# One layer of a four-layer gated stack on Trainium2: query projections placed ahead of scores, rounded rows transposed half a step later, product rows scaled on other engines

## The chip, the cores and the metric

The kernel runs on one core of a Trainium2 chip. The core has a matrix engine (TensorE, PE in the profile, with PEld for its weight loads), a vector engine (VectorE, DVE), an activation engine (ScalarE, ACT), a general-purpose engine (GpSimd, POOL) and a queue for transfers (SyncE, SP). Each engine executes its own instructions in the order in which the program lists them, and they wait for each other by semaphores. The metric is the device time of one execution in microseconds; the time before is 1705.65 us, the median of 3 runs (1699.48 to 1706.13).

## The reference, cut to what matters

Four layers, each an attention over a context and then a feed-forward part, are added to the rows x (8 batches of 256 rows with 128 features) behind a gate. The change touches layer 1:

```
# attention, per batch: 16 heads of 64, 256 queries, 512 keys
query = einsum('btd,dnh->bnth', q, w_query) + b_query
scores = einsum('bnth,bnsh->bnts', query, key_p) * scale
weights = softmax(scores, axis=-1)
attn = einsum('bnts,bnsh->bnth', weights, value)
out = einsum('bnth,ndh->btd', attn, w_projection) + b_projection
x = x + tanh(g_xattn[1]) * out           # q is layernorm(x)

# feed-forward: a product of rows and weights rounded to int8
lhs_scale = max(max(abs(lhs), axis=2), 1e-12) / 127      # per row
q_lhs = clip(round(lhs / lhs_scale), -127, 127)
acc = q_lhs @ q_rhs
x = x + tanh(g_ffn[1]) * (acc * lhs_scale * rhs_scale)   # lhs is layernorm(x)
```

## The kernel before

**The pipeline.** Layers 1 to 3 are one software pipeline (`pipeline`, L921). A unit is half the heads of one batch of one layer; there are 48 units, and each takes 4 steps. A step has two half steps, called A and B here. Three generators are advanced in step with each other: `prepare` (queries, operands) runs ahead by 8 steps, `largest` (row maxima of layers 2 and 3) by 4, and `attend` does the attention itself. Layer 1's preparation is done in steps 0 to 63 and its attention in steps 8 to 71, so both run together in steps 8 to 63. Work that is not tied to a half step waits in lists: `due` (run in A from the given step on), `soon` (run later in the same half step), and `front` and `back`, from each of which one piece is taken per half step (`some`, L1002). All instructions are kept in program order (`InOrder`, L36, and `mm` and `tp`, L866 to 873), so the order of the calls is the order on each engine.

**Layer 1's attention.** A half step handles one chunk of 128 queries for a pair of heads (`attend`, L1194). In order: the transposes of the weights of the chunk of two half steps ago, if there is one (`turn`, L994, which runs the function that `turned`, L1218, returns: 8 TensorE transposes into a buffer sc, ScalarE's copy into et, GpSimd's two additions k and total); this chunk's scores into another sc (two halves); VectorE's negated row maximum nm; and at the end of the half step ScalarE's two exponentials into a tile that the profile calls m (`exponentials`, L987). After both chunks of a pair have been transposed, the product with the values goes into av in the next A (`values_of_pair`, L1253). In the same half step the column sums follow, by ones, into av, then VectorE's reciprocal rec and the product aT. Of sc there are three buffers, of av one, and of pj one.

**The queries.** In B, after the scores, `prepare1` (L1142) projects the queries of a unit two units ahead into pj (the group pj<-xT,wb), and ScalarE copies them with the bias into qx.

**Row work of layer 1.** When a batch's eight pairs are done, `output1` (L1280) projects them through pj, adds them to x, and appends `int8(b)` (L1312) to `back`. That generator's pieces, one per half step, begin in an A: layernorm in four pieces (statistics on VectorE, the inverse root on GpSimd, the rows xn on VectorE), the scale of each row (ls and its inverse li), the rounding of one chunk of 128 rows (`rounded`, L1298: two VectorE operations r and one on GpSimd, ql), that of the other, then the transposes of ql into pj with ScalarE's copy qlT, an empty piece, and last the product pj<-qr,qlT. The product's pieces in the code before:

```
for c in range(2):
    nc.vector.scalar_tensor_tensor(
        y[:, c, :], po[:, c * D : (c + 1) * D], ls[:, c : c + 1], self.rsb,
        ALU.mult, ALU.mult,
    )
self.added(y, 2 * b)
```

Here y is the tile that the profile calls row, and rsb holds the weights' scale times the gate, the same for all rows. `added` (L1575) adds y to x on GpSimd. In `front`, `ahead` (L1062) prepares the next batch of layer 1: gathers by GpSimd, additions, layernorm, and `rows_turned` (L1073), which transposes xn through pj into xT. For layers 2 and 3 `ahead23` (L1080) does the like, and the pieces `project`, `values`, `mask`, `largest_rows` and `output23` use pj too.

Of the kernel before, what the change touches and what calls it, by code (L numbers as in the profile page):

```python
# [15 lines left out]
AF = mybir.ActivationFunctionType  # L16
ALU = mybir.AluOpType
AX = mybir.AxisListType

P = 128  # L20
NB, S, SK, D = 8, 256, 512, 128
# [10 lines left out]
def bcast(ap, shape):  # L32
    return ap.to_broadcast(list(shape))
# [15 lines left out]
class Flamingo:  # L49
# [871 lines left out]
    def pipeline(self):  # L921
        nc, tc = self.nc, self.tc
        with ExitStack() as st:
            PS = bass.MemoryType.PSUM
            self.p_sc = st.enter_context(tc.tile_pool(name="p_sc", bufs=3, space=PS))
            self.p_pj = st.enter_context(tc.tile_pool(name="p_pj", bufs=1, space=PS))
            self.p_av = st.enter_context(tc.tile_pool(name="p_av", bufs=1, space=PS))
            self.po = st.enter_context(tc.tile_pool(name="pipe", bufs=2))
            units = [(layer, b, g) for layer in (1, 2, 3) for b in range(NB) for g in range(2)]
            self.turns, self.exps = [], []  # L930
            self.due, self.soon, self.back, self.front, self.step, self.kept = [], [], [], [], 0, {}
            streams = {
                n: self.chain(f, units, wait)
                for n, f, wait in (("pr", self.prepare, 0), ("la", self.largest, 4), ("at", self.attend, 8))
            }
            self.fill_tile = lambda: self.t(self.po, "et", [P, 2, 2, S], bufs=6).rearrange(
                "p a b s -> p (a b s)"
            )[:, 0:SK]
            self.fill2(8)
            for _ in self.ahead(1, 0):  # L940
                pass
            for self.step in range(4 * len(units) + 12):

                next(streams["at"])
                self.run_due()
                next(streams["la"])
                self.run_soon()
                self.some(self.front)
                self.some(self.back)
                self.exponentials()  # L950
                next(streams["at"])
                next(streams["pr"])
                next(streams["la"])
                self.fill2(1)
                self.some(self.front)
                self.some(self.back)
                self.exponentials()
            while self.due or self.back:
                self.step += 1
                self.run_due()  # L960
                self.run_soon()
                self.some(self.back)
            self.ternary_end()
# [27 lines left out]
                self.nc.scalar.activation(p[:, z, :], ps[:, z, :], AF.Exp, bias=nm[:, z : z + 1])  # L991
        self.exps = []

    def turn(self, n):  # L994

        if len(self.turns) >= n:
            self.turns.pop(0)()

    def later(self, steps, f):
        self.due.append((self.step + steps, f))  # L1000
# [193 lines left out]
    def attend(self, n, layer, b, g):  # L1194
        if layer > 1:
            yield from self.attend23(n, layer, b, g)
            return
        nc = self.nc
        qT, kT, va = self.kept[n]
        aT = self.t(self.po, "aT", [P, 4, S], bufs=3)  # L1200
        self.kept["aT", g] = aT
        both = [self.kept["aT", 0], aT]
        for j in range(4):
            held = {}
            for c in range(2):
                self.turn(2)
                ps = self.sc()
                for z in range(2):
                    h = slice(64 * z, 64 * z + 64)
                    self.mm(ps[:, z, :], qT[h, j, c * P : (c + 1) * P], kT[h, j, :])  # L1210
                nm = self.t(self.po, "nm", [P, 2])
                nc.vector.tensor_reduce(nm, ps, AX.X, ALU.max, negate=True)
                p = self.t(self.po, "m4", [P, 4, S], bufs=3).rearrange("p (z k) s -> p z (k s)", z=2)
                self.exps.append((p, ps, nm))
                self.turns.append(self.turned(c, p, held, (b, 4 * g + j, va, both)))
                yield

    def turned(self, c, p, held, of_pair):  # L1218
# [93 lines left out]
    def int8(self, b):  # L1312
        nc = self.nc
        xn = self.t(self.po, "xn", [P, 2, D])
        yield from self.layernorm(2 * b, xn, self.nc.vector)
        ls = self.t(self.sm, "ls", [P, 2])
        li = self.t(self.sm, "li", [P, 2])
        self.absmax_scale(ls, li, xn)
        yield
        ql = self.t(self.po, "ql", [P, 2, D], BF16)  # L1320
        for c in range(2):
            self.rounded(ql[:, c, :], xn[:, c, :], li[:, c : c + 1], -127.0, 127.0)
            yield
        pt = self.pj16()
        for c in range(2):
            self.tp(pt[:, c * P : (c + 1) * P], ql[:, c, :], self.identb)
        qlT = self.t(self.po, "qlT", [P, S], BF16)
        nc.scalar.copy(qlT, pt[:, 0:S])
        yield
        yield  # L1330
        po = self.pj()
        y = self.t(self.rows, "row2", [P, 2, D])
        for c in range(2):
            self.mm(po[:, c * D : (c + 1) * D], qlT[:, c * P : (c + 1) * P], self.qr)
        for c in range(2):
            nc.vector.scalar_tensor_tensor(
                y[:, c, :], po[:, c * D : (c + 1) * D], ls[:, c : c + 1], self.rsb,
                ALU.mult, ALU.mult,
            )
        self.added(y, 2 * b)  # L1340


# [142 lines left out]
    def attend23(self, n, layer, b, g):  # L1485
        qx, kx, _ = self.kept[n]
        va = self.kept["va", layer, b]
        _, bk = self.kept["mask", layer, b]
        rows = 38 if layer == 2 else 34
        scale = 1.0 / math.sqrt(8.0) if layer == 2 else 128.0**-0.5  # L1490
        if g == 0:
            aT = self.t(self.po, "aT", [P, 4, S], bufs=3)
            self.kept["oS"] = aT[:, 0:2, :], aT[:, 2:4, :]
        oS, oN = self.kept["oS"]
        held = {}
        for j in range(4):
            for k2 in range(2):
                self.turn(1)
                ps = self.sc()
                for z in range(2):  # L1500
                    self.mm(
                        ps[:, z, :], self.identb,
                        bk[:, 2 * k2 : 2 * k2 + 2, :].rearrange("p k s -> p (k s)"), True, False,
                    )
                for c in range(2):
                    for z in range(2):
                        at = (2 * k2 + c) * P
                        self.mm(
                            ps[:, z, c * S : (c + 1) * S],
                            self.packed(kx, z, 0, rows)[:, j, at : at + P].bitcast(F32R),  # L1510
                            self.packed(qx, z, 0, rows)[:, j, :].bitcast(F32R), False, c == 1,
                        )
                held[j, k2] = self.weights(ps, scale)
                if k2 and j % 2:
                    self.later(1, self.values_of_four(layer, b, g, j // 2, held, va, oS, oN))
                yield
# [340 lines left out]
```

## Time and profile before

| | |
|---|---|
| median of 3 runs | 1705.65 us (1699.48 to 1706.13) |
| profiled execution | 1706.16 us, its span 1704.4 us |
| busy: TensorE | 1501.9 us, 88% of the span |
| busy: VectorE | 1135.8 us, 67% |
| busy: ScalarE | 891.8 us, 52% |
| busy: GpSimd | 737.9 us, 43% |
| mean granted TensorE clock | 0.950 |
| layer 1's attention | about 345 to 875 us |
| a plain step in it (transposes at 601.96 and at 609.04) | 7.08 us |
| its five whole batches, 400 to 760 us: TensorE busy | 338.64 of 360 us |
| the same: VectorE, ScalarE, GpSimd busy | 253.57, 214.43, 227.49 us |

Names like `pj<-xT,wb` say which tile is written from which; buffer numbers are left out. A bracket or a column "idle before" gives the time that the engine had nothing to do ahead of an instruction, and the engine and tile whose end released it. The granted clock is the share of the TensorE clock that the chip let through in a stretch.

### The profile page before, as it was taken

What the parts mean: (1) busy time and instruction counts of PE and PEld (TensorE: products, weight loads), DVE (VectorE), ACT (ScalarE), POOL (GpSimd) and SP (SyncE); (2) the same over time, 40 slices, a digit from 0 to 9 for tenths busy, and PEclk for the clock granted to TensorE, in tenths of its full rate; (3) what the DMA queues carried; (4) which work ended last, traced back from release to release, by engine and by line L of the source; (5) the groups of instructions that cost most, each with busy time, mean ns of one, the idle gap of its engine ahead of it and who ended that gap; (6) DMA issues with size and microseconds to landing.
All of it is one profiled execution on the core that took longest, in us unless ns stands there. A gap on an engine that the chain in (4) does not pass through costs nothing.

```text
span 1704.4 us, 33649 instructions
## 1 busy us (share of the span) xinstructions
PE 1501.9 (88%) x12560; PEld 801.6 (47%) x12560; DVE 1135.8 (67%) x2634; ACT 891.8 (52%) x1468; POOL 737.9 (43%) x1189
## 2 busy tenths in 40 slices
PE   5886778799899999999888898898899999899995
PEld 2332225256566565566553444444444455344442
DVE  6998652156776767767776765664755755677764
ACT  3453443466555556556444555555555455455543
POOL 5896312355665766666542132222322323433311
PEclk9898998999999999999999999999999899899997
DMA  5453442731221122122222331222211121222200
GB/s 200 149 174 122 160 163 94 245 119 53 80 73 59 58 79 76 57 75 71 43 90 71 81 72 48 53 58 50 60 34 46 45 54 28 60 60 61 61 21 26
DMA packets 64903, 137.54 MB, mean 81 GB/s; under 512 B 12114, under 2 KB 27619, under 8 KB 58084
## 3 DMA queue, kind: packets, MB, share of 16 engines
q1 hardware_dynamic: 62770, 131.70, 25.2%
q0 software_dynamic: 1536, 3.15, 1.1%
q8 instruction: 100, 1.64, 0.4%
q10 hardware_dynamic: 434, 0.54, 0.1%
q14 instruction: 63, 0.52, 0.1%
HBM read 83.44 MB, written 51.38 MB: 79 GB/s over the span
## 4 chain that ended last, share of the span: by engine, by line
PE 56%; DVE 14%; ACT 6%; issue 6%; POOL 5%; DMA 2%; SPq 1%; ACTq 0%; DVEq 0%; POOLq 0%
PE sc L868 26%; PE av L868 14%; PE pj L868 7%; PE sc L872 5%; DVE junk L46 5%; PE pj L872 3%; DVE rec L46 2%; ACT et L46 1%; DVE x L46 1%; POOL lnz L46 1%; ACT total L46 1%; ACT m L46 1%; DVE nm L46 1%; POOL xs L46 1%; ACT row L46 1%
## 5 line engine op out<-in xcount | busy, mean ns | idle before, releaser
L46 DVE CUSTOM_DVE_ANT_0 junk<-sc,m 128x512 bf16<-128x512 f32 x512 | 350.8, 685 | 44.2 <-PE sc L868 30.7
L46 ACT ACTIVATE et<-sc 128x1024 f32<-128x1024 f32 (+1 forms) x267 | 268.9, 1008 | 147.4 <-PE sc L868 142.6
L868 PE MATMUL sc<-kx,qx 64*128 64x512 f32 (+2 forms) x1024 | 272.0, 571 | 7.1 <-DVE mx L46 5.3
L868 PE MATMUL av<-et,va 128*64 128x128 f32 (+1 forms) x4096 | 268.0, 348 | 0.0
L868 PEld LDWEIGHTS av<-et,va 128*64 128x64 f32 (+1 forms) x4096 | 178.7, 129 | 96.3 <-issue 49.7
L46 POOL TENSOR_TENSOR k<-et 128x512 f32<-128x512 f32 x128 | 162.7, 1271 | 131.2 <-ACT et L46 130.5
L46 ACT ACTIVATE m<-sc,nm 128x512 f32<-128x512 f32 x256 | 162.1, 685 | 88.6 <-DVE nm L46 86.2
L46 DVE TENSOR_REDUCE nm<-sc 128x2 f32<-128x1024 f32 x128 | 156.2, 1220 | 65.5 <-PE sc L868 57.4
L868 PE MATMUL sc<-m,identb 128*128 128x512 bf16 x512 | 159.9, 395 | 19.9 <-DVE mx L46 11.9
L46 POOL TENSOR_TENSOR x<-row,x 128x256 f32<-128x256 f32 x76 | 55.4, 729 | 268.1 <-ACT row L46 262.5
L46 ACT COPY et<-sc 128x1024 f32<-128x1024 f32 x128 | 129.7, 1013 | 60.5 <-PE sc L872 60.4
L46 DVE RECIPROCAL rec<-av 128x256 f32<-128x256 f32 x64 | 112.3, 1754 | 53.6 <-PE av L868 53.6
L872 PE MATMUL sc<-c_f,m 128*128 128x128 f32 x1024 | 139.1, 279 | 3.4 <-ACT m L46 2.9
L868 PE MATMUL sc<-qx,kx 38*128 38x256 f32 (+1 forms) x1024 | 133.6, 340 | 0.4 <-DMA qx<-ms 0.4
L868 PEld LDWEIGHTS sc<-qx,kx 38*128 38x128 f32 (+1 forms) x1024 | 79.5, 192 | 114.7 <-issue 111.4
L872 PEld LDWEIGHTS sc<-c_f,m 128*128 128x128 f32 x1024 | 110.3, 141 | 45.9 <-issue 35.6
L868 PEld LDWEIGHTS sc<-kx,qx 64*128 64x128 f32 (+2 forms) x1024 | 87.8, 187 | 73.3 <-issue 45.9
L46 DVE SCALAR_TENSOR_TENSOR x<-sc,comb,x 128x128 f32<-128x128 f32 x128 | 39.0, 346 | 100.3 <-ACT row L46 100.3
L46 POOL TENSOR_TENSOR lnz<-lny 128x2 f32<-128x2 f32 (+1 forms) x129 | 25.1, 195 | 183.5 <-DVE lny L46 169.8
L46 ACT ACTIVATE total<-sc,f_b 128x512 f32<-128x512 f32 x64 | 44.0, 688 | 107.5 <-PE sc L868 107.5
L46 POOL TENSOR_TENSOR total<-k 128x256 f32<-128x256 f32 x128 | 93.2, 728 | 10.0
L46 DVE SCALAR_TENSOR_TENSOR ms<-pj,ms 4x256 fp32r<-4x256 f32 x64 | 26.4, 412 | 100.8 <-ACT ms L46 93.0
(274 smaller groups left out, 2319.2 us busy)
## 6 DMA issues: line engine op xcount, KB each, us to landing
kx<-k SPq DMA_DIRECT2D x16, 1024.0 KB
va<-v SPq DMA_DIRECT2D x16, 1024.0 KB
k<-fill SPq DMA_DIRECT2D x54, 256.0 KB
v<-fill SPq DMA_DIRECT2D x53, 256.0 KB
pd<-k SPq DMA_DIRECT2D x16, 512.0 KB
kx<-pd SPq DMA_DIRECT2D x64, 128.0 KB
kx<-pd SPq DMA_DIRECT2D x128, 64.0 KB
qx<-pd SPq DMA_DIRECT2D x128, 64.0 KB
```

What stands on the lines that cost most here:

```text
L46: return lambda *args, **kw: self.tc.keep_in_program_order(v(*args, **kw))
L868: self.nc.tensor.matmul(out, lhsT, rhs, start=start, stop=stop)
L872: self.tc.keep_in_program_order(self.nc.tensor.transpose(out, in_, ident))
```

## The change

Three things are changed. First, the transposes are called by the pipeline itself at the head of each half step, and in steps 0 to 63 the B half step advances `pr` (the queries) before `at` (the scores); from step 64 on `at` comes first as before. `turn` now keeps one entry per half step, empty where there is nothing to transpose, and runs the one of two half steps ago. Second, `int8` has one more empty piece between the rounding and the transposes of ql, so that these, qlT and the product each come a half step later, in the other kind of half step. Third, the product's rows are multiplied by the row's scale on ScalarE, reading pj, and by rsb on GpSimd, where VectorE did both in one operation per chunk.

```
@@ pipeline
             for self.step in range(4 * len(units) + 12):
 
+                self.turn()
                 next(streams["at"])
                 self.run_due()
                 next(streams["la"])
...
                 self.exponentials()
-                next(streams["at"])
-                next(streams["pr"])
+
+                self.turn()
+                for n in ("pr", "at") if self.step < 8 * NB else ("at", "pr"):
+                    next(streams[n])
                 next(streams["la"])
@@
-    def turn(self, n):
-
-        if len(self.turns) >= n:
-            self.turns.pop(0)()
+    def turn(self):
+
+        self.turns.append(None)
+        if len(self.turns) > 2 and (run := self.turns.pop(0)):
+            run()
@@ attend
             for c in range(2):
-                self.turn(2)
                 ps = self.sc()
...
-                self.turns.append(self.turned(c, p, held, (b, 4 * g + j, va, both)))
+                self.turns[-1] = self.turned(c, p, held, (b, 4 * g + j, va, both))
                 yield
@@ int8
             self.rounded(ql[:, c, :], xn[:, c, :], li[:, c : c + 1], -127.0, 127.0)
             yield
+        yield
         pt = self.pj16()
...
         for c in range(2):
-            nc.vector.scalar_tensor_tensor(
-                y[:, c, :], po[:, c * D : (c + 1) * D], ls[:, c : c + 1], self.rsb,
-                ALU.mult, ALU.mult,
+            nc.scalar.activation(
+                y[:, c, :], po[:, c * D : (c + 1) * D], AF.Copy, scale=ls[:, c : c + 1]
             )
+        nc.gpsimd.tensor_tensor(y, y, bcast(self.rsb.unsqueeze(1), [P, 2, D]), ALU.mult)
         self.added(y, 2 * b)
@@ attend23
             for k2 in range(2):
-                self.turn(1)
                 ps = self.sc()
```

## The prediction

> **What bounds the kernel now.** I read the page first, then the PE's list of waits, the PE's timeline of one batch, and the table of stretches for the granted clock.
>
> ```profile
> PE 1501.9 (88%) x12560; PEld 801.6 (47%) x12560; DVE 1135.8 (67%) x2634; ACT 891.8 (52%) x1468; POOL 737.9 (43%) x1189
> PE 56%; DVE 14%; ACT 6%; issue 6%; POOL 5%; DMA 2%; SPq 1%; ACTq 0%; DVEq 0%; POOLq 0%
> ```
>
> TensorE is 88% busy and is over half of the chain that ended last. Layer 1's attention runs from 345 to 875 us, so that is the stage to read. Its waits on PE between 400 and 760 us, which is five batches (the columns are the total, the count and the longest):
>
> ```profile
> PE pj L872 <- ACT qx L46: 6.8, 10, 0.8
> PE pj L872 <- POOL ql L46: 5.3, 5, 1.1
> PE sc L872 <- ACT m L46: 2.9, 5, 0.6
> PE pj L868 <- ACT qx L46: 2.9, 5, 0.6
> PE pj L872 <- DVE xn L46: 2.5, 5, 0.5
> PE av L868 <- POOL total L46: 1.1, 5, 0.2
> ```
>
> Each comes a whole number of times per batch, so one batch tells all. Its places, from PE's timeline of the third batch (start, duration, what; the bracket is the idle time before it):
>
> ```profile
> 574.70 1.09 PE L872 MATMUL sc<-c_f,m 128*128 128x128 f32 x8 [0.58 <-ACT m L46]
> 575.72 1.13 PE L868 MATMUL sc<-kx,qx 64*128 64x512 f32 x4
> 576.78 0.65 PE L868 MATMUL pj<-xT,wb 128*64 128x256 f32 x4
> 578.21 0.22 PE L872 MATMUL pj<-identb,ql 128*128 128x128 bf16 x1 [0.78 <-ACT qx L46]
> 579.48 0.23 PE L872 MATMUL pj<-identb,ql 128*128 128x128 bf16 x1 [1.05 <-POOL ql L46]
> ...
> 588.84 0.27 PE L868 MATMUL pj<-qr,qlT 128*128 128x128 bf16 x2 [0.57 <-ACT qx L46]
> ...
> 596.62 0.33 PE L872 MATMUL pj<-c_f,xn 128*128 128x128 f32 x1 [0.57 <-ACT qx L46]
> 597.44 0.33 PE L872 MATMUL pj<-c_f,xn 128*128 128x128 f32 x1 [0.49 <-DVE xn L46]
> ```
>
> There is one pj buffer. Whatever writes it right behind the queries waits until ScalarE has read them (qx). Outside these places PE has no idle time over 0.1 us: a plain step is 7.08 us (transposes at 601.96 and again at 609.04).
>
> The granted clock, in stretches of 3.41 us laid on the grid of its drops (columns: length, PE busy, PEld, DVE, ACT, POOL, clock, DMA):
>
> ```profile
> 512.26:515.67 3.41, 1.99 (x14) 1.18 (x13) 2.77 (x9) 1.82 (x5) 2.28 (x3) 1.00 0.00 0
> 515.67:519.08 3.41, 3.41 (x45) 2.70 (x44) 1.87 (x2) 2.20 (x4) 2.21 (x3) 1.00 0.02 5
> 577.12:580.53 3.41, 1.58 (x16) 0.98 (x12) 3.27 (x10) 1.82 (x4) 2.22 (x3) 1.00 0.21 87
> 580.53:583.94 3.41, 3.41 (x19) 1.91 (x20) 1.42 (x3) 1.66 (x3) 2.45 (x4) 0.50 0.00 0
> ```
>
> Where both waits of the int8 transposes (0.78 and 1.05) fall into one stretch, PE is busy for 1.58 of 3.41 us and the next stretch runs at half clock. Where they are split (busy 1.99, and 2.30 from 645.38) it does not. Stretches starting at 444.00 and 710.24 are like 577.12: 1.58 busy, then 0.50. From the second int8 transposes to the first row transposes a batch with such a drop takes 17.14 us (579.48 to 596.62), one without 15.52 (513.89 to 529.41): a drop costs 1.62 us.
>
> **The sum's base.** The profiled execution: 1706.16 us (span 1704.4 and 1.8 around it), 0.5 above the median 1705.65.
>
> **Queries ahead of scores, 56 half steps (steps 8 to 63).** No instruction is added; in the built order PE alone changes places. Queries take 0.59 us start to start (576.78's group, from 604.04 to 604.63), scores 1.06. So qx is read while the scores run, and a writer of pj behind the scores finds it free: the three 0.57-type waits go. What is queued behind the queries is now the scores: they end 0.59 us later after their transposes, and with them their maximum (nm, 1.22), their exponentials (m, 1.27) and the copy of the next et. In a plain step the exponentials end at 606.75 (605.49 and 1.26) and the transposes that read them start at 609.04: 2.29 us, of which 1.70 stay. The smallest in a place where scores and not VectorE set the time is 1.51, leaving 0.92. I cost this at nothing; that slack covers it.
>
> **Rounded rows a half step later.** The extra yield puts the transposes of ql behind the ones matmuls of the next half step, 4.4 us of PE work later (transposes 1.02, scores 1.06, values 1.80, ones 0.53). ql ended at 579.42, so both waits (0.78, 1.05) go. The parity also flips: transposes and product now stand in half steps without queries. What is late next: the totals of GpSimd, 581.46 against ones that would start at 581.3 (574.70 and 2.67 for a half step, then 1.02, 1.06 and 1.80), so a wait of about 0.2. The exponentials of that half step stand behind the qlT copy (0.37) on ScalarE; their slack was 3.71.
>
> **Product's rows.** VectorE loses 16 x 0.341 us, 0.68 per batch. ScalarE gains 16 scaled reads; the nearest row is the same form from sc, 128x128 at 363 ns. GpSimd gains 8 multiplications of 128x256, nearest x<-row,x and x<-x,bias at 0.73. Behind the two scaled reads stand the exponentials of that half step: ones end at t, product t+0.3, reads t+1.05, exponentials t+2.4; transposes that read them come at t+2.8 (product 0.12, transposes 1.02, queries 0.59, scores 1.06). Queries need pj at t+1.14. Both fit, by 0.4 and 0.1 us: nothing taken, at most 0.5 per batch. On GpSimd the next k waits behind 0.73 us more; its total is due over 2 us after it. No DMA moves but one load of kx on SP, behind four of qx, in layer 2: the same five issues, at nothing.
>
> **Row transposes (xn).** Their 0.57 goes, but the second waits for VectorE: from the end of ones (593.38) 1.75 rec, 0.42 aT, 1.83 for two xn, 4.06 in all. PE now has 2.8 to 3.1 us of work in that gap, the product included. If the xn stay as long, about 1.0 us of waiting is left of 1.06, less the product's 0.12; the xn ranged from 0.34 to 1.30 us, and with short ones nothing is left.
> [...]
>
> **Sum for batches 1 to 5.** From 574.70 to 597.61 is 22.91 us, 21.29 without its clock drop. Removed waits are 0.78+1.05+0.57+0.57+0.49 = 3.46; what comes back is 0.2 and 0 to 1.0 before xn. Kept: 2.6 to 3.4, I take 2.9: 14.5 us. Three clock drops at 1.62: 4.9 (0 to 4.9). In the new order no stretch holds more than about 1.0 us of waiting, and 1.42 (busy 1.99) did not drop the clock.
>
> **Batches 6 to 8** overlap layer 2's preparation, where the flipped parity meets other users of pj. Sixth: 0.57 at 777.88 goes; the product's 0.57 at 785.66 turns into a wait for the xT copy (0.37 and 0.09): 0.7 (0 to 1.1). Seventh: 0.41 and 0.86 go at 845 and 846, the scaled reads get ahead of exponentials for which PE already waited 1.40 at 868.37: 0 (-1.0 to 1.3). Eighth: waits of 1.78, 0.85 and 1.27 (904.49, 905.56, 916.29) go, 0.8 come back (ms and xT hold pj), and VectorE is busy without a pause there: 2.1 (1.0 to 3.1). Its two stretches at half clock from 904.80 follow one with PE busy 1.54: 1.7 (0 to 3.4).
>
> Sum: 14.5 + 4.9 + 0.7 + 0 + 3.8 = 23.9; 1706.2 - 23.9 = **1682.3 us**.
>
> **Rivals.**
> *The clock drops come back.* Drops at 447.41, 580.53 and 713.65 stand 133.1 apart, so they could belong to a rhythm and not to the stalls. Then 4.9 and 1.7 are not gained: 1689. Against it: they follow exactly the three stretches with PE under 1.6 us busy. 0.14.
> [...]
> *VectorE sets the pace.* It works without a pause from 564.33 to 580.75, through all of the int8 part, so PE would wait at its next transposes instead and the idle stretch, with its drop, stays. Only the product's 5 x 0.57 and the sixth batch's 0.7 are gained: 1702.6. Against it: it then idles for 1.96 us for scores (582.71), and the transposes that need its last maximum have 4.24 us of slack. 0.08.
> *Slower: the softmax loop closes.* Scores 0.59 later decide if the exponentials' slack in plain steps is under that: each of 56 steps pays up to 0.59, 33.0 us: 1682.3 + 33.0 = 1715. Against it: the 2.29. For it: ScalarE copies et only behind those exponentials. 0.06.
>
> **Numbers.** Forecast 0.68, clock 0.14, VectorE 0.08, slower 0.06; 0.04 for part gains between these times. A measurement of this kernel tells about 0.5% from no change: faster is under 1697. Faster 0.86 (forecast, clock, part gains), same 0.08, slower 0.06. The low end takes every upper bound: 17.0 + 4.9 + 1.1 + 1.3 + 6.5 = 30.8, 1675, and 1 for drops elsewhere, whose place moves with time: the three runs before already differ by 6.6. The high end takes the clock rival with 2.6 per batch and the low bounds of the last three, 13.0 in all, 1693, and 3 for drops elsewhere: 1696. With the two cases inside, the range leaves out under 2 in 10.
>
> **What would show it.** Right: in the waits on PE, ACT qx and POOL ql gone from the steps with attention in layer 1, a plain step still 7.08 us, no half clock between 430 and 740, vector rows gone. Wrong: PE waiting for ACT m in plain steps, pj waiting for ACT row, or half-clock stretches beside a busy PE.

## The result, and the profile after

The changed kernel takes 1690.01 us, the median of 8 runs (1684.51 to 1692.53). The kernel before, run beside it, takes 1705.89 (8 runs, 1699.48 to 1716.16). The ratio is 0.9903 with a 95% interval of 0.9877 to 0.9929: faster by 0.97%, or 15.9 us. The forecast was 23.9 us (1682.3); the direction is right, the time lies in the range, and two thirds of the gain came. By the whole time alone this could not be told from the rival in which the clock drops come back, whose time was 1689; the traces below tell the two apart.

The profiled execution after took 1692.39 us (span 1690.6), against 1706.16 before, 13.8 less. First the line of busy times on the page after. TensorE is as busy a share as before; VectorE lost 5.9 us, ScalarE lost 1.1 in spite of its 16 new reads, GpSimd gained 8.6:

```profile
PE 1495.2 (88%) x12464; PEld 803.0 (47%) x12560; DVE 1129.9 (67%) x2618; ACT 890.7 (53%) x1484; POOL 746.5 (44%) x1197
```

TensorE's waits between 400 and 740 us after, which holds five batches again (total, count, longest). Six groups of before are three, and 21.5 us are 6.2:

```profile
PE pj L872 <- ACT qx L46: 3.2, 5, 0.6
PE sc L872 <- ACT m L46: 1.8, 3, 0.6
PE av L868 <- POOL total L46: 1.2, 5, 0.2
```

The places, from TensorE's timeline of the third batch after. Queries (pj<-xT,wb) now stand ahead of scores; the transposes of ql and the int8 product follow the ones without a wait; what is left is 0.63 us ahead of the row transposes, besides the 0.59 for m, which was 0.58 before:

```profile
568.42 1.09 PE L872 MATMUL sc<-c_f,m 128*128 128x128 f32 x8 [0.59 <-ACT m L46]
569.44 0.65 PE L868 MATMUL pj<-xT,wb 128*64 128x256 f32 x4
570.02 1.13 PE L868 MATMUL sc<-kx,qx 64*128 64x512 f32 x4
...
575.24 0.65 PE L868 MATMUL av<-total,ones 128*64 128x256 f32 x4
575.83 0.29 PE L872 MATMUL pj<-identb,ql 128*128 128x128 bf16 x2
...
582.98 0.28 PE L868 MATMUL pj<-qr,qlT 128*128 128x128 bf16 x2
...
586.42 0.45 PE L872 MATMUL pj<-c_f,xn 128*128 128x128 f32 x2 [0.63 <-ACT qx L46]
```

Two neighbouring batches, in stretches between the same instructions (columns: length, then busy time of PE, PEld, DVE, ACT, POOL, then granted clock, DMA share, GB/s). Before, then after:

```profile
433.62:500.80 67.18, 62.91 (x582) 40.34 (x582) 47.40 (x64) 39.57 (x58) 42.75 (x64) 0.97 0.20 67
500.80:566.39 65.59, 61.32 (x582) 39.65 (x583) 47.38 (x64) 39.57 (x58) 42.75 (x64) 1.00 0.21 69
```

```profile
498.46:560.10 61.64, 60.76 (x582) 39.52 (x583) 45.45 (x62) 39.06 (x60) 43.52 (x65) 1.00 0.23 74
560.10:622.75 62.65, 61.07 (x583) 39.52 (x583) 46.49 (x62) 39.07 (x60) 43.55 (x65) 1.00 0.23 72
```

A batch at full clock went from 65.59 to 62.65, or to 61.64 where VectorE is busy 1.04 us less (by one operation on ls, see the last section). A stretch at clock 0.97 holds one drop; after, none of the five batches has one.

Where the 13.8 us of the two profiled executions came from, by stages that end at the same instruction in both:

| stage | before | after | difference | forecast |
|---|---|---|---|---|
| start to the first scores of layer 1 (same code) | 344.79 | 347.87 | +3.1 | 0 |
| to the reciprocal of the 4th pair | 35.18 | 34.23 | -1.0 | 0 |
| to that of the 52nd pair: batches 1 to 5 | 393.83 | 372.24 | -21.6 | -19.4 (14.5 and 4.9) |
| to the first rec<-rec of layer 2: batches 6 to 8 | 156.23 | 158.09 | +1.9 | -4.5 (0.7, 0, 3.8) |
| to the fourth rec<-rec (same code) | 155.80 | 160.87 | +5.1 | 0 |
| to the end | 618.57 | 617.29 | -1.3 | 0 |

So batches 1 to 5 gave 2.2 us more than forecast, and all the other stages, for which 4.5 were forecast, took 7.8 more in sum.

### The profile page after: what moved, and what is told of

It is laid out like the page before. It is cut to its first block, busy times and chain, and to the rows that moved or that the text cites. A ratio compares the mean times of both kernels' runs of the same rounds, so it can differ in the third digit from the quotient of the medians.

```text
span 1690.6 us, 33565 instructions
## 1 busy us (share of the span) xinstructions
PE 1495.2 (88%) x12464; PEld 803.0 (47%) x12560; DVE 1129.9 (67%) x2618; ACT 890.7 (53%) x1484; POOL 746.5 (44%) x1197
## 4 chain that ended last, share of the span: by engine, by line
PE 56%; DVE 13%; ACT 6%; POOL 6%; issue 6%; DMA 1%; SPq 0%; ACTq 0%; DVEq 0%; POOLq 0%
PE sc L868 26%; PE av L868 14%; PE pj L868 8%; DVE junk L46 6%; PE sc L872 5%; PE pj L872 3%; POOL lnz L46 2%; ACT et L46 2%; DVE rec L46 1%; POOL k L46 1%; DVE x L46 1%; ACT m L46 1%; ACT row L46 1%; ACT total L46 1%; DVE nm L46 1%
## 5 line engine op out<-in xcount | busy, mean ns | idle before, releaser
L868 PE MATMUL sc<-m,identb 128*128 128x512 bf16 x416 | 140.6, 403 | 22.9 <-DVE mx L46 12.4
```

Of the source, the lines that this page charges most:

```text
L868: self.nc.tensor.matmul(out, lhsT, rhs, start=start, stop=stop)
```

## The experiments

Three theories were to be told apart. *Waits*: each wait that goes is worth its own length, and the clock drops belong to the stalls at ql. *Clock rhythm*: the drops come on their own. *Closed loop*: the later exponentials, or VectorE, set the pace. Each kernel has the kernel before run beside it; in the first four its median was 1710.62 us (26 runs), in the others, on another chip, 1721.62 (11 runs). Where a time is compared below, it is by the ratio to those. "The five batches" is the stage to the 52nd reciprocal of the table, less its first eight pairs, which take 62.8 us in all kernels but the last. The hand-over is the stage behind it, with batches 6 to 8.

**Order of queries and scores alone.** As after, with the two other parts undone:

```
@@ int8
-        yield
         pt = self.pj16()
...
-            nc.scalar.activation(y[:, c, :], po[:, c * D : (c + 1) * D], AF.Copy, scale=ls[:, c : c + 1])
-        nc.gpsimd.tensor_tensor(y, y, bcast(self.rsb.unsqueeze(1), [P, 2, D]), ALU.mult)
+            nc.vector.scalar_tensor_tensor(
+                y[:, c, :], po[:, c * D : (c + 1) * D], ls[:, c : c + 1], self.rsb, ALU.mult, ALU.mult)
```

> Only the order of queries and scores in steps 8 to 63 is changed; the rounded rows and the product stay as before. Measure: the long stretch of 48 pairs from the fourth reciprocal rec<-av to the fifty-second (393.8 us before, 372.2 with the whole change), and the hand-over from there to the first rec<-rec of layer 2 (156.2 before, 158.1 with the whole change). My theory (each part removes its own waits): the product's 0.57 goes per batch, the int8 transposes still wait for ql at the same time, so idle time and clock drops stay: long stretch 389 to 391, hand-over 156, whole time 1701 to 1705. Rival (the order does it all): long stretch under 378, whole time under 1693. Rival (softmax loop closes): plain step 7.6 instead of 7.08, long stretch over 410.

Measured: 1700.43 us (5 runs), ratio 0.9937 (0.9903 to 0.9971). A batch at full clock takes 64.38, 1.2 less than before. TensorE's timeline of it: the product's wait is gone, the two at ql stay as long as they were, and the two at xn, 0.57 and 0.49 before, are 0.09 and 0.41:

```profile
574.29 0.22 PE L872 MATMUL pj<-identb,ql 128*128 128x128 bf16 x1 [0.78 <-ACT qx L46]
575.56 0.23 PE L872 MATMUL pj<-identb,ql 128*128 128x128 bf16 x1 [1.05 <-POOL ql L46]
...
590.67 0.33 PE L872 MATMUL pj<-c_f,xn 128*128 128x128 f32 x1 [0.41 <-DVE xn L46]
```

The long stretch took 384.56 us, against 389 to 391 expected and under 378 for the first rival. So the order is worth 1.2 per batch, twice what was expected: it frees pj at xn too, with the row work left where it was. And with the stalls at ql unchanged, only one of five batches shows a drop, not three. Stretches of this kernel on the grid of its drops (columns as above):

```profile
636.30:639.71 3.41, 1.81 (x9) 0.47 (x9) 3.31 (x7) 2.32 (x4) 2.14 (x3) 1.00 0.60 255
639.71:643.13 3.42, 3.19 (x33) 2.27 (x35) 2.34 (x6) 2.44 (x4) 2.54 (x4) 1.00 0.02 5
...
701.16:704.57 3.41, 1.58 (x10) 0.63 (x9) 3.31 (x7) 1.83 (x3) 2.14 (x4) 1.00 0.45 187
704.57:707.98 3.41, 3.41 (x12) 1.64 (x10) 0.94 (x5) 2.55 (x4) 2.34 (x3) 0.50 0.00 0
```

The same two stalls leave TensorE busy 1.81 us in one stretch and 1.58 in another, by where the grid's edge cuts them; only the second is followed by half clock.

**The extra empty piece alone.** The kernel before with one line added:

```
@@ int8
             self.rounded(ql[:, c, :], xn[:, c, :], li[:, c : c + 1], -127.0, 127.0)
             yield
+        yield
         pt = self.pj16()
```

> Only the extra empty piece: ql's transposes, qlT and the product a half step later, in half steps without queries; the product's rows still on VectorE. My theory: the waits 0.78, 1.05 and 0.57 go, but the product's rows now stand on VectorE behind rec, aT and the two xn (4.0 us), pj stays taken until then, and the next queries wait some 2.3 us in one piece: long stretch 388 to 398, a halved clock behind most of these pieces. Rival (the empty piece alone brings most of the gain): long stretch under 382, no halved clock in it.

Measured: 1708.65 us (10 runs), ratio 0.9988 (0.997 to 1.0007). A batch at full clock takes 64.00, 1.6 less than before; the stalls at ql are gone, and this comes in their place:

```profile
591.31 0.65 PE L868 MATMUL pj<-xT,wb 128*64 128x256 f32 x4 [1.39 <-DVE row L46]
592.54 0.69 PE L872 MATMUL pj<-c_f,xn 128*128 128x128 f32 x2 [0.57 <-ACT qx L46]
```

The queries wait until VectorE has read the product out of pj. Two of five batches still have a clock drop. The long stretch took 384.28 us, less than the 388 to 398 expected, as the wait was 1.39 and not 2.3. The 1.6 per batch are there, yet the whole time is that of before. In the profiled execution the hand-over to layer 2 took 161.78 us instead of 156.23, with seven stretches at half clock instead of three, and the stage of unchanged code behind it 162.40 instead of 155.80, with six instead of one.

**The rows alone.** The kernel before with the product's rows on ScalarE and GpSimd, on the old order:

```
@@ int8
-            nc.vector.scalar_tensor_tensor(
-                y[:, c, :], po[:, c * D : (c + 1) * D], ls[:, c : c + 1], self.rsb, ALU.mult, ALU.mult)
+            nc.scalar.activation(y[:, c, :], po[:, c * D : (c + 1) * D], AF.Copy, scale=ls[:, c : c + 1])
+        nc.gpsimd.tensor_tensor(y, y, bcast(self.rsb.unsqueeze(1), [P, 2, D]), ALU.mult)
```

> Only the product's rows on ScalarE and GpSimd. My theory: VectorE's 0.68 us per batch was beside other work, and ScalarE's 0.73 fits into slack: long stretch 393 to 395, nothing gained; hand-over 155 to 158. Rival (VectorE sets the pace of the int8 part): 0.7 per batch gained, long stretch 389 to 390.

Measured: 1708.16 us (10 runs), ratio 0.9983 (0.9967 to 0.9998). A batch at full clock takes 65.19, 0.4 less, between the nothing that was expected and the 0.7 of the rival. VectorE does not reach the xn sooner, it waits for TensorE ahead of rec as before (1.04 us there); the second xn takes 0.88 us instead of 1.30, and TensorE's wait there went from 0.49 to 0.08. The long stretch took 388.59 us, with two drops fewer than before. The stalls at ql stand in every batch, and again only one of the five drops the clock.

**All but the rows.** The changed kernel, its empty piece kept, with the rows on VectorE:

```
@@ int8
-            nc.scalar.activation(y[:, c, :], po[:, c * D : (c + 1) * D], AF.Copy, scale=ls[:, c : c + 1])
-        nc.gpsimd.tensor_tensor(y, y, bcast(self.rsb.unsqueeze(1), [P, 2, D]), ALU.mult)
+            nc.vector.scalar_tensor_tensor(
+                y[:, c, :], po[:, c * D : (c + 1) * D], ls[:, c : c + 1], self.rsb, ALU.mult, ALU.mult)
```

> The whole change but the product's rows, which stay on VectorE. My theory: rows behind rec, aT and xn hold pj for about 4.7 us after ones, and queries, which now stand ahead of the scores, wait for some 3.4 us in one piece: of the 14.5 us in five batches nearly all is given back, the clock halves behind each piece: long stretch 388 to 400, whole time 1698 to 1712. Rival (who does the rows is of no weight): long stretch 371 to 374, whole time 1690.

Measured: 1711.44 us (10 runs), ratio 0.9995 (0.9971 to 1.0018). The wait comes where it was expected, with 2.43 us instead of 3.4, and the long stretch of 390.63 us lies in the range; the rival is false. Queries ahead of scores run straight into the product's buffer. The waiting queries on TensorE, then VectorE, where the rows stand last, behind rec (and aT and xn, which are left out here):

```profile
595.89 0.73 PE L868 MATMUL pj<-xT,wb 128*64 128x256 f32 x4 [2.43 <-DVE row L46]
```

```profile
592.41 1.76 DVE L46 RECIPROCAL rec<-av 128x256 f32<-128x256 f32 x1 [1.04 <-PE av L868]
...
595.24 0.59 DVE L46 SCALAR_TENSOR_TENSOR row<-pj,ls,rsb 128x128 f32<-128x128 f32 x2
```

A batch at full clock takes 64.41, and four of the five have a drop, one of them two. So the rows, worth 0.4 alone, are worth 1.8 a batch and the drops beside the other two parts: they keep the new wait away. The parts one by one are worth 1.2, 1.6 and 0.4 per batch at full clock, 3.2 in sum; all three at once are worth 2.9.

**All but the empty piece.** The changed kernel without the second yield in int8:

```
@@ int8
             yield
-        yield
         pt = self.pj16()
```

> The whole change without the extra empty piece: queries ahead of scores and the product's rows on ScalarE and GpSimd, but ql's transposes as early as before. My theory: per batch the drop-free gains of the parts add up, 1.2 us for the order and 0.4 for the rows as measured alone, and the waits 0.78 and 1.05 stay: a batch without a clock drop 64.0 us (65.6 before, 62.65 with the whole change), and a drop in a batch only where one stretch of 3.41 us on the clock's grid has PE busy for under 1.65 us. Rival (the empty piece is of no weight once the order is changed): 62.7 per batch, no wait for ql.

Measured: 1714.53 us (1 run; before 1721.62). Batches take 65.23, 65.22, 65.24, 64.18 and 63.42, 1.2 above what was expected for most: waits of 0.92 and 0.42 are left at the row transposes. That is 0.85 more than with the order alone, so beside the order the moved rows cost time unless the empty piece is there too. The first xn takes 1.25 us here and ends at 605.75, just behind GpSimd's k (605.67), which the new multiplication had put later; with the order alone it took 0.43. TensorE's waits between 400 and 740 us:

```profile
PE pj L872 <- DVE xn L46: 7.0, 11, 0.9
PE pj L872 <- POOL ql L46: 5.3, 5, 1.1
```

The two stalls at ql stand in all five batches, and none drops the clock.

**Later exponentials.** The changed kernel with a copy that nobody reads, ahead of the exponentials of each half step with queries:

```
@@ pipeline
                 self.some(self.back)
+                if 8 <= self.step < 8 * NB:
+                    late = self.t(self.po, "late", [P, 1024], BF16, bufs=1)
+                    self.nc.scalar.copy(late, self.ctxT[:, 0:1024])
                 self.exponentials()
```

> The whole change, with one more ScalarE copy of 128x1024 ahead of the exponentials of each half step with queries in steps 8 to 63 (some 1.0 us; its result is not used). It moves these exponentials and the next copy of et later, as the scores moved them by 0.59. My theory: 1.70 us of slack in plain steps carries it; plain step stays 7.08, long stretch 372 to 378. Rival (the softmax loop is nearly closed): plain step 7.5 to 8.1, long stretch over 390.

Measured: 1702.72 us (1 run; before 1721.62), the long stretch 373.97 us, the five batches 311.19 against 309.42 for the change itself. The 1.8 more need not be the copy's: VectorE's operation on ls (last section) was short in two batches of the change's profile and in none here, and the next kernel, without the copy and also without a short one, took 311.16. The plain step is 7.08 as before, from TensorE's timeline, though ScalarE's has the copy ahead of the exponentials:

```profile
604.50 1.09 PE L872 MATMUL sc<-c_f,m 128*128 128x128 f32 x8
...
611.57 1.09 PE L872 MATMUL sc<-c_f,m 128*128 128x128 f32 x8
```

```profile
606.96 1.05 ACT L46 CAST late<-ctxT 128x1024 bf16<-128x1024 f32 x1
608.61 1.26 ACT L46 ACTIVATE m<-sc,nm 128x512 f32<-128x512 f32 x2 [0.60 <-DVE nm L46]
```

The second line shows that this test is weaker than meant: ScalarE still waited 0.60 for VectorE's maximum, so the copy filled idle time and did not delay the exponentials of this step. That the loop has slack is read from the traces themselves: in the changed kernel the exponentials of a plain step end at 596.44 and the transposes that read them start at 598.14, 1.70 later, as forecast.

**The last two batches as before.** The changed kernel with the empty piece and the moved rows only for the first six batches:

```
@@ int8
-        yield
+        if b < 6:
+            yield
...
+        if b < 6:
+            for c in range(2):
+                nc.scalar.activation(
...
+        else:
+            for c in range(2):
+                nc.vector.scalar_tensor_tensor(
...
```

> The empty piece and the rows on ScalarE and GpSimd only for the first six batches; the last two, whose int8 parts run beside layer 2, stay as before. The order of queries and scores as in the whole change. My theory (in the last two batches the flipped half step costs what it saves): long stretch 372, hand-over 155 to 157 against 158.1. Rival (the hand-over's 1.9 us more is the clock's phase alone): hand-over 158 or spread to both sides of it without a new pattern of waits.

Measured: 1698.76 us (4 runs), ratio 0.9884 (0.9855 to 0.9914). The hand-over took 155.10, with two stretches at half clock, against 158.09 with four after. Waits of before are back in it, 0.86 for ql at 838.48 and 2.42 for mx at 850.53. The expected 155 to 157 was met, but less its stretches at half clock the hand-over is as long as after (table below), so the rival, the clock's phase alone, is not refuted.

**One more empty piece, ahead of the row transposes.** The kernel of the last experiment with one line more, to take the last 0.63:

```
@@ ahead
         self.biased(b, self.bias[layer])
+        yield
         self.rows_turned(layer, b, xn)
```

> As first_six, and the next batch's row transposes (xn) one half step later, in one without queries. My theory: the 0.63 that PE waits there for ScalarE's qx goes, and nothing comes back, since the next queries that need xT stand a half step and 1.0 us of transposes later: batches of 62.0 us against 62.65, long stretch 368 to 370, whole time 0.988 of before. Rival (that wait only hides VectorE's): the wait moves to xT or xn, long stretch 372.

Measured: 1699.53 us (6 runs), ratio 0.9878 (0.985 to 0.9907). The wait at the row transposes is gone and the five batches take 305.89, 3.5 less than after; but the hand-over took 163.76 with seven stretches at half clock. The ratios of this kernel, of the last and of the change itself (0.9903) overlap: no version here is shown to beat the change.

## Why the prediction was right, and where its sizes were off

**The waits, 14.5 for batches 1 to 5: right.** Without their three drops, at 1.62 each, the five batches took 326.2 us before and took 309.42 after: 16.8 less. Three batches gave 2.9 to 3.0, the 2.9 that was taken; two gave 4.0. Those two are the ones with the short operation on ls (last section), which was no term of the sum; without its 2.0 us the waits brought 14.8. The kernels with the later exponentials and with the last two batches as before, in which no such operation was short, took 311.2, 15.0 less.

Of the 3.46 per batch that were to go, 0.11 to 0.13 came back at the new place behind GpSimd's totals (575.24), in three batches, where 0.2 was forecast. The 0.2 for totals in both lists of waits is another place (566.39 before), which the prediction left out when it said that there is no idle time over 0.1 us outside its places. And 0.63 came back at the row transposes, where 0 to 1.0 was forecast for VectorE's xn. There two causes end almost together, 0.12 us apart: ScalarE's qx at 586.36, which was not named, and the second xn at 586.49. That xn took 0.77 us beside GpSimd's new multiplication (from 585.68, 0.73 long), against 0.33 in the kernel with all but the rows. With either cause alone most of the wait would probably have stayed; the last experiment moved the transposes behind both. ScalarE's timeline after shows how qx became late: the two scaled reads wait for the product, and the exponentials, et and the reading of the queries stand behind them:

```profile
583.30 0.63 ACT L46 ACTIVATE row<-pj,ls 128x128 f32<-128x128 f32 x2 [1.12 <-PE pj L868]
583.82 1.27 ACT L46 ACTIVATE m<-sc,nm 128x512 f32<-128x512 f32 x2
584.96 1.03 ACT L46 COPY et<-sc 128x1024 f32<-128x1024 f32 x1
585.85 0.51 ACT L46 ACTIVATE qx<-pj,bq 128x256 f32<-128x256 f32 x1
```

The prediction had named this queue for the product's half step and found that it fits by 0.1 us for the queries; it did not follow the queue on to qx, which the row transposes wait for.

**The clock drops, 4.9: the cause right, the size one execution's luck.** The three drops are gone and no stretch between 430 and 740 is at half clock, as forecast. In the stage from 400 to 760 us of all traces, the stretches that were followed by half clock had TensorE busy for 0.97 to 1.62 us of 3.41; one with 1.66 was not:

```profile
657.78:661.19 3.41, 1.66 (x18) 1.04 (x12) 2.77 (x4) 1.89 (x3) 2.78 (x7) 1.00 0.01 2
661.19:664.60 3.41, 2.72 (x18) 1.57 (x18) 1.53 (x4) 0.84 (x2) 2.62 (x3) 1.00 0.04 10
```

This is from the kernel with all but the rows; the kernel with the rows alone has the nearest on the other side:

```profile
705.41:708.82 3.41, 1.62 (x12) 1.18 (x13) 3.14 (x10) 1.83 (x5) 2.14 (x4) 1.00 0.07 29
708.82:712.23 3.41, 3.41 (x24) 2.10 (x22) 1.23 (x1) 1.96 (x4) 2.53 (x3) 0.50 0.00 0
```

So in this stage every drop followed a stretch with stalls, and the same stalls brought one or none by where the grid cuts them: busy 1.58 and a drop, busy 1.81 and none (order alone, above). With the same stalls, before had a drop in three of five batches, the three kernels that keep them had 1, 1 and 0: 5 in 20, which makes about 2.0 us per execution, not 4.9. Before's profile seems to have been an unlucky one in this stage; there is only one of it. The rival that the drops come back is false for batches 1 to 5: the gain there holds without them. The longest gap of TensorE in these batches before, with the three drops in it, was 1.05 us. The grid is read from the granted clock: the three stretches at half clock before are 3.41 us long and start at 447.41, 580.53 and 713.65, each 133.12 us after the last, which is 39 times 3.413.

**Batches 6 to 8, 4.5 in all: wrong.** The waits that were counted did go, and others took their place. The hand-over, split at the 59th and 63rd reciprocal into the stretches with the sixth, seventh and eighth batch's places:

| stretch | before | after | gain | forecast | at half clock before, after |
|---|---|---|---|---|---|
| sixth | 56.60 | 57.07 | -0.5 | 0.7 | 0, 0 |
| seventh | 43.31 | 46.05 | -2.7 | 0 | 1, 3 |
| eighth | 56.32 | 54.97 | 1.4 | 3.8 | 2, 1 |

In the sixth the two waits of 0.57 went and the 0.46 for xT came, as forecast. But the queries, now earlier, also run into another user of pj, VectorE's reading of k, which the prediction had not counted. TensorE's timeline after:

```profile
757.22 0.65 PE L868 MATMUL pj<-xT,wb 128*64 128x256 f32 x4 [1.03 <-DVE k L46]
```

In the seventh the waits of 0.41, 0.86 and 0.76 are now one of 1.87, and 2.42 became 1.99. TensorE's timeline before, then after:

```profile
846.24 0.23 PE L872 MATMUL pj<-identb,ql 128*128 128x128 bf16 x1 [0.86 <-POOL ql L46]
...
848.11 1.13 PE L868 MATMUL sc<-kx,qx 64*128 64x512 f32 x4 [0.76 <-ACT m L46]
```

```profile
829.03 1.13 PE L868 MATMUL sc<-kx,qx 64*128 64x512 f32 x4 [1.87 <-ACT m L46]
...
840.84 2.08 PE L868 MATMUL sc<-kx,qx 64*128 64x512 f32 x4 [1.99 <-DVE mx L46]
```

VectorE binds there. It works without a pause from 821.87 to 829.36 after, and through the same instructions from 840.95 to 848.44 before, 7.49 us in both, with the maximum nm 4.53 us from the first in both; TensorE's waits for pj only hid a part of the wait for that nm. VectorE's timeline before, then after, the first of the stretch and this nm:

```profile
840.95 0.69 DVE L46 CUSTOM_DVE_ANT_0 junk<-sc,m 128x512 bf16<-128x512 f32 x1 [2.35 <-PE sc L868]
...
845.48 1.22 DVE L46 TENSOR_REDUCE nm<-sc 128x2 f32<-128x1024 f32 x1
```

```profile
821.87 0.69 DVE L46 CUSTOM_DVE_ANT_0 junk<-sc,m 128x512 bf16<-128x512 f32 x1 [1.59 <-PE sc L868]
...
826.40 1.22 DVE L46 TENSOR_REDUCE nm<-sc 128x2 f32<-128x1024 f32 x1
```

And the waits, now in one piece, leave TensorE busy for 1.54 us of a stretch and for 1.56 of another, from 837.13, each followed by half clock (the first of them in after, columns as above):

```profile
826.89:830.30 3.41, 1.54 (x11) 0.55 (x11) 2.43 (x8) 2.17 (x3) 2.78 (x7) 1.00 0.42 159
830.30:833.72 3.42, 3.42 (x34) 2.99 (x30) 1.20 (x1) 0.00 (x0) 3.01 (x8) 0.50 0.00 0
```

In the eighth the waits of 1.78, 0.85 and 1.27 went. From the same projection (pj<-ctxT,wp) to the same transposes (pj<-identb,m) TensorE took 21.42 us before (900.43 to 921.85), with two stretches at half clock, and 20.05 after (884.20 to 904.25), with one. Its waits of over 0.3 us in between add up to 4.7 before and 4.2 after. The two longest of before, then of after:

```profile
904.49 0.22 PE L872 MATMUL pj<-identb,ql 128*128 128x128 bf16 x1 [1.78 <-DVE k L46]
...
916.29 0.41 PE L872 MATMUL pj<-c_f,xn 128*128 128x128 f32 x2 [1.27 <-DVE row L46]
```

```profile
887.43 0.59 PE L868 MATMUL sc<-m,identb 128*128 128x512 bf16 x2 [0.94 <-ACT et L46]
...
898.63 1.01 PE L868 MATMUL sc<-m,identb 128*128 128x512 bf16 x2 [0.95 <-ACT et L46]
```

What was gained there is about one stretch at half clock; which engine binds is not shown, as VectorE has pauses in it after (1.57 us ahead of 897.73).

At 1.62 for each stretch at half clock, the hand-over without drops is 150.4 to 153.2 in these kernels, 151.4 before and 151.6 after; at the 1.3 that such a stretch costs in the next stage (below) it is 152.3 and 152.9. So the waits that went gained nothing there.

| kernel | hand-over | stretches at half clock | less 1.62 each | next stage (same code) | its stretches at half clock |
|---|---|---|---|---|---|
| before | 156.23 | 3 | 151.4 | 155.80 | 1 |
| after | 158.09 | 4 | 151.6 | 160.87 | 5 |
| order alone | 156.08 | 3 | 151.2 | 159.84 | 4 |
| empty piece alone | 161.78 | 7 | 150.4 | 162.40 | 6 |
| rows alone | 157.74 | 4 | 151.3 | 161.78 | 5 |
| all but the rows | 158.03 | 3 | 153.2 | 157.19 | 2 |
| all but the empty piece | 155.89 | 3 | 151.0 | 159.85 | 4 |
| later exponentials | 156.61 | 3 | 151.8 | 157.22 | 2 |
| first six batches | 155.10 | 2 | 151.9 | 156.06 | 1 |
| first six and one more piece | 163.76 | 7 | 152.4 | 160.15 | 4 |

The rival "VectorE sets the pace" was refused by the slack of one plain batch; in batches 1 to 5 that held, in the seventh batch the rival is right. The step that failed is the 4.5 for batches 6 to 8, above all the 3.8 for the eighth: waits were added up one by one, less what came back at the same buffer, in a stage where other waits take their place, although the prediction itself saw VectorE busy without a pause in the eighth. The 0 for the seventh holds but for its drops. Whether the two drops of after at 830 and 840 belong to the change or to chance stays open: the profile with the later exponentials, which holds the whole change too, has two in the same places, at 843.2 and 853.5 of its own span, but it is only one more.

**The rest of the program, 0: wrong as the difference of two profiles.** The stage from the first to the fourth rec<-rec is the same code, and it went from 155.80 to 160.87. Here it is before and then after (columns as above; the last but two is the granted clock):

```profile
930.03:1085.83 155.80, 141.53 (x1310) 71.95 (x1306) 100.33 (x313) 84.18 (x147) 39.38 (x89) 0.99 0.27 66
```

```profile
912.44:1073.31 160.87, 144.64 (x1291) 74.03 (x1306) 101.08 (x313) 84.68 (x147) 39.55 (x89) 0.95 0.27 64
```

The other engines' work is within 1% of equal, the clock is not: 0.99 against 0.95, one stretch at half clock against five. In the table this stage goes with the count of such stretches, at about 1.3 us each, and not with the parts of the change, and before's profile is the shortest of them, by 3.7 us against the mean of the other nine. So the profile the sum was made against was probably lucky here by some 4 us, and unlucky by some 3 in layer 1. The prediction allowed 3 us at the high end for drops elsewhere; this stage and the first one, also the same code, moved by 8.2 together.

**The sum again.** With 14.8 for the waits of batches 1 to 5, 2.0 for drops at their mean rate, and nothing for batches 6 to 8 less the one extra drop of 1.6, 15.2 us come out, and 17.2 with the short operations on ls, against 15.9 between the medians. This is an account from these runs, not a separate measurement. The forecast was 8 us too fast, of which 4.5 are batches 6 to 8 and 2.9 the drops; the time lies in the range because its high end had left out the drops and most of batches 6 to 8.

**The slower rival** is false by the unchanged plain step and its 1.70 us of slack.

**The expectations that missed** did so the same way: a wait was followed to the one place where it shows, not to the next (order alone: 1.2 for 0.57; all but the empty piece: more left at xn), or the time of VectorE's xn was taken from before: 1.83 for two, where they took under 0.8 in these two kernels, so that the rows behind them started sooner (2.43 for 3.4, 1.39 for 2.3).

## What to carry to other kernels

A wait on the bounding engine was worth its length here where no other engine worked through the same time without a pause (14.8 us came for the 14.5 in batches 1 to 5), and nothing where VectorE did (7.49 us in the seventh, before and after): ask that again in every stage, and distrust a sum of single waits in a stage with two bounds. Count a clock drop seen in one profile at its mean rate: here the same stalls brought one in 3 of 5 batches of one profile, and in 1, 1 and 0 of 5 of three others. Compare stages of identical code in the two profiles first: what they differ by is the error of everything else that is read from one pair.

## What was not expected of the hardware

In layer 1's batches (400 to 760 us, ten traces) the drops of the clock went with how long TensorE was busy in a stretch of 3.41 us, not with the length of a gap: the eleven stretches with 1.62 us or less were followed by one at half clock, those at full clock with 1.66 or more were not, and the drop cost 1.62 us where it was measured in one batch (17.14 against 15.52). Gaps of 0.78 and 1.05 us, both in one stretch (busy 1.58 from 577.12 before), were followed by half clock, and the same gaps cut by the grid (busy 1.99 from 512.26) were not. The profile's busy time does not tell all: in the hand-over and the stage behind it, some stretches at full clock with more were followed by half clock too (1.89 from 986.72 before, 2.43 from 936.12 and 2.79 from 977.07 after), and one with 2.14, from 843.36 before, was not.

VectorE's operation on ls, of 128x2 elements, has two durations in the same place of the same program. It took 1.98 us in all five whole batches before. After, it took 1.98 in three and 0.17 in two, and those two batches are the 1.0 us shorter ones; TensorE's 0.59 us of waiting for m stands in the three and not in the two. Both cases start 0.31 us after GpSimd began an indirect transfer (563.43 and 501.80) and 0.67 or 0.68 before its k. VectorE's timeline after, first the short and then the long one:

```profile
502.11 0.17 DVE L46 TENSOR_SCALAR ls<-ls 128x2 f32<-128x2 f32 x1
...
563.74 1.98 DVE L46 TENSOR_SCALAR ls<-ls 128x2 f32<-128x2 f32 x1
```

The long one ends at 565.72 with GpSimd's k (565.69), so it looks held by GpSimd's work; what lets the other through was not tried and stays open, and so does whether the change has a part in it: of the eight other changed kernels six have only long ones there, that without the empty piece has one short one and the last three.
